# Exponentials and weighted sums over whole rows of 4096 columns, with the broadcast rows in single tiles refilled by halves

## The chip, the cores and the metric

The kernel runs on one core of one Trainium2 chip. The metric is device time in microseconds (us) for one execution, as a median of runs; lower is better. A profile of one execution gives each engine's instructions and waits: TensorE (PE, with its weight loads PEld), VectorE (DVE), ScalarE (ACT), GpSimd (POOL) and SyncE (SP), which issues most of the DMAs.

## The reference, cut to what matters

The input is 16 images of 64 x 64 positions with 256 channels, 4096 tokens an image. Four layers follow each other, each normalized per group of channels over the image, and each added to its input. Layer 0 replaces each token by the nearest of 1024 codes (the "search"). Layer 1 is a gated attention inside each image row. Layer 2, where the change lies, makes three scalars x0, x1, x2 per token, a 4096 x 4096 similarity, its softmax, and a gate:

```python
def layer2(x, w1, b1, w2, b2, w3, b3):
    x0 = jnp.einsum('bnc,c->bn', xf, w1) + b1[0]
    x1 = jnp.einsum('bnc,c->bn', xf, w2) + b2[0]
    x2 = jnp.einsum('bnc,c->bn', xf, w3) + b3[0]
    sim = x0[:, :, None] * x1[:, None, :]
    sm = jax.nn.softmax(sim, axis=1)
    feats = jnp.einsum('bn,bnm->bm', x2, sm)
    gate = jax.nn.sigmoid(feats).reshape(b, h, w, 1)
    return gate * x
```

For each of the 4096 tokens m, the sum over n of exp(x0[n] x1[m]) and the sum of the same weighted by x2[n] are needed. Layer 3 is a linear attention with four heads, an output projection and a layer norm.

## The kernel before, in words

The program is written as Python generators, one for each stage of each image: stats0 and stage1 (search), layer1, rows2 (the three scalars), stage2 (the exponentials), gate2 (the gate is applied) and stage3 (layer 3). A heap of due times (the list `tasks` at the end of the kernel) decides which generator is advanced next, so that at any time several images are in different stages; each `yield` gives a share of the stage's length, and one image takes about as long as one stage of exponentials. A scheduler below the language then sets the order of instructions on each engine by priority and readiness, inserts the waits, and gives out the buffers. Within one engine instructions run in that order.

rows2(b) loads the image's eight chunks again (L562, tile xr), multiplies them on TensorE by the three weight vectors (L565), copies the row to SBUF (L569), writes it to DRAM (`rd`, L571) and turns x0 and x1 into one column per 128 tokens (x01, L575). `spread_rows` (L582 to L590) then brings one half row, 2048 columns of x0 and of x2, back to all 128 partitions (x0b and x2b, two buffers each, 1 MB a transfer, issued on SP's queue at L587). The first half is spread at the end of rows2, the second at the start of stage2.

stage2(b) takes the extremes of x0 over partitions (L598 to L601, with a GpSimd reduction), makes the bias nmax from them (L603, L604), and then runs 64 halves: for each half row and each of 32 groups of 128 tokens, ScalarE makes the exponentials of 2048 columns and their sum den (L617), into one of three buffers `ex`, and VectorE multiplies them by x2b and sums them into num (L620). Both read a per-partition scalar or two and write an accumulator. Then den and num of the two halves are added and the gate is formed (L628 to L641). The last image runs with parts=8: 8 groups of four tokens' groups, with its gate2 stage interleaved.

The search (stage1) makes for each of the 32 token groups T the row of norms `nn` on ScalarE (L372), the products with the 1024 codes on TensorE into a PSUM tile of 1024 columns (pd, L377, from the pool ps_w with two buffers), their sum with nn and its maximum on VectorE (L384, into `nd`), the index of the maximum (L389), and a gather of codes by GpSimd (L390). The 4 KB tiles nn, nd, the squares sq (L320), fg of layer 1 (L461) and rows share one tag, t4, with five buffers. The other PSUM tiles come from a pool of four banks (ps_m), which all stages share. Other lines that are named later: L468 and L506 are layer 1's products, L511 its sum on VectorE, L857 and L865 the scaled copy and the sum at layer 3's output.

Of the kernel before, what the change touches and what calls it, by code (L numbers as in the profile page):

```python
# [9 lines left out]
F32 = mybir.dt.float32  # L10
BF16 = mybir.dt.bfloat16
U32 = mybir.dt.uint32
AF = mybir.ActivationFunctionType
ALU = mybir.AluOpType
AX = mybir.AxisListType

P = 128
C = 256
NK = C // P
TOK = 4096  # L20
NT = TOK // P
CH = 4
NCHUNK = NT // CH
CW = CH * P
# [3 lines left out]
CODES = 1024  # L28
CK = 32
# [12 lines left out]
def kernel(  # L42
# [7 lines left out]
    nc = tc.nc  # L50
# [8 lines left out]
    s1p = ctx.enter_context(tc.tile_pool(name="s1p", bufs=2))  # L59
    s2p = ctx.enter_context(tc.tile_pool(name="s2p", bufs=1))  # L60
    s3p = ctx.enter_context(tc.tile_pool(name="s3p", bufs=2))
    wts = ctx.enter_context(tc.tile_pool(name="wts", bufs=1))
    small = ctx.enter_context(tc.tile_pool(name="small", bufs=2))
# [34 lines left out]
    neg_mat = s1p.tile([P, P], F32, tag="t4", name="neg_mat", bufs=5)  # L98
# [72 lines left out]
    e_raw = s2p.tile([P, NK, CODES], F32, tag="x0b", name="e_raw", bufs=2)  # L171
# [3 lines left out]
    e_sq = s2p.tile([P, NK, CODES], F32, tag="x2b", name="e_sq", bufs=2)  # L175
# [127 lines left out]
    def stage1(b):  # L303
        tag = f"s1_{b}"
        scale, _, nbias = norm0.pop(b)
# [12 lines left out]
        def norm(ch):  # L318
            xn[ch] = s1p.tile([P, NK, CW], F32, tag="xn", name=f"xn_{tag}_{ch}")
            sq = s1p.tile([P, NK, CW], F32, tag="t4", name=f"sq_{tag}_{ch}", bufs=5)  # L320
            for k in range(NK):
                nc.scalar.activation(
                    xn[ch][:, k, :], xt[ch][:, k, :], AF.Identity, bias=nbias[:, k : k + 1], scale=scale[:, k : k + 1]
                )
                nc.scalar.activation(
                    sq[:, k, :], xt[ch][:, k, :], AF.Square, bias=nbias[:, k : k + 1], scale=scale[:, k : k + 1]
                )
            px = bank(f"px_{tag}_{ch}")
            for t in range(CH):
                for k in range(NK):  # L330
                    nc.tensor.matmul(
                        px[32 * t : 32 * t + 32, :P], lhsT=neg32, rhs=sq[:, k, t * P : (t + 1) * P],
                        start=(k == 0), stop=(k == NK - 1),
                    )
            xrow = small.tile([P, P], F32, tag="xrow", name=f"xrow_{tag}_{ch}", bufs=1)
            nc.scalar.copy(xrow, px[:, :P])
            pxt[ch] = bank(f"pxt_{tag}_{ch}")
            nc.tensor.transpose(pxt[ch][:, :P], xrow, ident)
# [28 lines left out]
        for ch in range(NCHUNK):  # L367
            for t in range(CH):
                T = ch * CH + t

                nn = s1p.tile([P, CODES], F32, tag="t4", name=f"nn_{tag}_{T}", bufs=5)
                nc.scalar.activation(nn, ne2, AF.Identity, bias=nx2[ch][:, t : t + 1])  # L372
                pd = wide(f"pd_{tag}_{T}")
                for hf in range(2):
# [7 lines left out]
                nd = s1p.tile([P, CODES], F32, tag="t4", name=f"nd_{tag}_{T}", bufs=5)  # L382
                m8 = m8s[T % 4]
                nc.vector.tensor_tensor_reduce(  # L384
                    out=nd, in0=pd, in1=nn, scale=1.0, scalar=-3.0e38, op0=ALU.add, op1=ALU.max,
                    accum_out=m8[:, 0:1],
                )
                i8 = small.tile([P, 8], U32, tag="i8", name=f"i8_{tag}_{T}", bufs=4)
                nc.vector.max_index(i8, m8, nd)  # L389
# [26 lines left out]
    def layer1(b):  # L416
# [34 lines left out]
        def attend(ch):  # L451
# [9 lines left out]
            fg = s1p.tile([2 * CK, 2, HW], F32, tag="t4", name=f"fg_{tag}_{ch}", bufs=5)  # L461
# [78 lines left out]
    def rows2(b):  # L540
# [17 lines left out]
        for h in range(2):  # L558
# [9 lines left out]
            rows = s1p.tile([P, CW], F32, tag="t4", name=f"rows_{tag}_{h}", bufs=5)  # L568
# [11 lines left out]
        rows_d[b] = x01, rd, [spread_rows(rd, b, 0)]  # L580

    def spread_rows(rd, b, h):  # L582

        x0b = s2p.tile([P, TOK // 2], F32, tag="x0b", name=f"x0b_{b}_{h}", bufs=2)
        x2b = s2p.tile([P, TOK // 2], F32, tag="x2b", name=f"x2b_{b}_{h}", bufs=2)
        for dst, n in ((x0b, 0), (x2b, 2)):
            nc.sync.dma_start(  # L587
                out=dst, in_=rd[n : n + 1, h, :, :].rearrange("o j n -> o (j n)").to_broadcast([P, TOK // 2])
            )
        return x0b, x2b  # L590

    def stage2(b, parts=1):

        tag = f"s2_{b}"
        x01, rd, halves = rows_d.pop(b)
# [6 lines left out]
        nmax = small.tile([P, NT], F32, tag="nmax", name=f"nmax_{tag}", bufs=1)  # L602
        nc.vector.tensor_scalar(nmax, x01[:, :, 1], ab[:, 0:1], -1.0, ALU.mult, ALU.mult)  # L603
        nc.vector.scalar_tensor_tensor(nmax, x01[:, :, 1], ab[:, 1:2], nmax, op0=ALU.mult, op1=ALU.min)  # L604
        den = small.tile([P, 2, NT], F32, tag="den", name=f"den_{tag}", bufs=1)
        num = small.tile([P, 2, NT], F32, tag="num", name=f"num_{tag}", bufs=1)
        halves.append(spread_rows(rd, b, 1))
# [3 lines left out]
        rest = gate2(b) if parts > 1 else None  # L611
        for part in range(parts):
            those = range(part * NT // parts, (part + 1) * NT // parts)
            for h, (x0b, x2b) in enumerate(halves):
                for T in those:
                    ex = s2p.tile([P, TOK // 2], F32, tag="ex", name=f"ex_{tag}_{h}_{T}", bufs=3)
                    nc.scalar.activation(  # L617
                        ex, x0b, AF.Exp, bias=nmax[:, T : T + 1], scale=x01[:, T, 1:2], accum_out=den[:, h, T : T + 1]
                    )
                    nc.vector.tensor_tensor_reduce(  # L620
                        out=ex, in0=ex, in1=x2b, scale=1.0, scalar=0.0, op0=ALU.mult, op1=ALU.add,
                        accum_out=num[:, h, T : T + 1],
                    )
                    yield 2.4
# [320 lines left out]
```

## Time and profile before

| What | Value |
|---|---|
| Median of three runs | 5938.17 us (5902.65 to 5948.46) |
| The profiled execution's own time | 5928.44 us |
| Its span in the profile | 5926.7 us |
| Busy: TensorE, VectorE, ScalarE, GpSimd | 5337.4, 5121.1, 4570.8, 1939.4 us |
| Granted TensorE clock, mean | 0.941 |
| DMA | 1059.47 MB, mean 179 GB/s |

The page gives busy time per engine, then the costliest groups of instructions by line: busy time and mean duration in nanoseconds of one, then the idle time of the engine just before them and who ended it. A table of stages gives the busy time of each engine (with its number of instructions) in a stretch of the span, then the granted clock, the share of time that the DMA engines were busy, and GB/s. The waits list who waited for whom: us in total, number of times, the longest. The timeline lists instructions by start and duration; the chain in order of time follows the end of the program back through what released each step.

### The profile page before, as it was taken

The numbers are of one execution on the slowest core, as the hardware profiler recorded it, in microseconds if no ns is written. First come the engines' busy times: TensorE is split into PE (matmuls) and PEld (weight loads), VectorE is DVE, ScalarE is ACT, GpSimd is POOL, SyncE is SP. The second block draws the span as 40 slices with busy tenths as digits, with TensorE's granted clock in tenths as the row PEclk, the third lists the DMA queues.
The fourth block names the chain that finished last, engine by engine and source line by source line (L and its number), as shares of the span: only waits on it lengthen the run. The fifth ranks groups of instructions, "written<-read, shape, count | busy, mean of one in ns | idle before, by whom it ended". The sixth has DMA issues, their size and how long they took to land.

```text
span 5926.7 us, 79561 instructions
## 1 busy us (share of the span) xinstructions
PE 5337.4 (90%) x28239; PEld 3211.1 (54%) x28239; DVE 5121.1 (86%) x7282; ACT 4570.8 (77%) x6754; POOL 1939.4 (33%) x1314
## 2 busy tenths in 40 slices
PE   8968899889999999998989999898999989997777
PEld 3524465545656565564656556565555646564555
DVE  6499798989989898898989889898998989888882
ACT  4377687878778787887879788797878878787873
POOL 3122233224233332433334233342424333231331
PEclk9989999989999898999999899999999999998899
DMA  6544745555656656565665656656565664644543
GB/s 186 162 124 124 225 137 177 184 184 162 207 168 192 197 151 202 184 207 181 184 205 167 194 183 188 206 174 204 164 210 164 202 204 147 209 158 173 184 158 116
DMA packets 521380, 1059.47 MB, mean 179 GB/s; under 512 B 52504, under 2 KB 266392, under 8 KB 512792
## 3 DMA queue, kind: packets, MB, share of 16 engines
q1 hardware_dynamic: 406288, 885.11, 44.7%
q0 software_dynamic: 73728, 67.14, 7.9%
q10 hardware_dynamic: 40968, 102.13, 4.5%
q8 instruction: 224, 3.67, 0.3%
q14 instruction: 172, 1.41, 0.1%
HBM read 751.18 MB, written 303.04 MB: 178 GB/s over the span
## 4 chain that ended last, share of the span: by engine, by line
PE 48%; DVE 16%; ACT 12%; DMA 7%; issue 6%; POOL 4%; ACTq 0%; SPq 0%; POOLq 0%; DVEq 0%
PE pd_s L377 15%; DVE ex_s L620 6%; ACT ex_s L617 5%; PE ph_l L468 5%; PE pqv_s L759 3%; PE po_s L854 3%; PE pk_s L737 3%; PE po_l L506 2%; PE pr_r L565 2%; DMA xr_r<-x_l 2%; DVE i_s L389 2%; POOL qv_s L779 2%; PE pvr_s L834 1%; PE pz_s L826 1%; DMA qo_s<-qd_s 1%
## 5 line engine op out<-in xcount | busy, mean ns | idle before, releaser
L620 DVE CUSTOM_DVE_ANT_0 ex_s<-ex_s,x2b 128x2048 f32<-128x2048 f32 x1024 | 2350.7, 2302 | 46.2 <-ACT ex_s L617 44.9
L617 ACT ACTIVATE ex_s<-x0b,nmax_s,x_r 128x2048 f32<-128x2048 f32 x1024 | 2137.8, 2088 | 66.4 <-DVE num_s L620 60.3
L377 PE MATMUL pd_s<-e,xn_s 128*128 128x512 f32 x4096 | 2022.2, 623 | 43.5 <-DVE m L384 40.8
L390 POOL DMA_INDIRECT xc_s<-in_emb_rows,i_s x512 | 1058.1, 2067 | 2063.9 <-DVE i_s L389 1466.8
L377 PEld LDWEIGHTS pd_s<-e,xn_s 128*128 128x128 f32 x4096 | 754.4, 197 | 764.9 <-issue 669.1
L384 DVE CUSTOM_DVE_ANT_0 nd_s<-pd_s,nn_s 128x1024 f32<-128x1024 f32 x512 | 622.2, 1215 | 174.4 <-ACT nn_s L372 82.1
L389 DVE FIND_INDEX8 i_s<-m,nd_s 128x8 uint32<-128x1024 f32 x512 | 624.1, 1219 | 0.0
L372 ACT ACTIVATE nn_s<-ne,nx_s 128x1024 f32<-128x1024 f32 x512 | 583.2, 1141 | 21.5 <-DVE nx_s L343 15.7
L468 PE MATMUL ph_l<-wh_l,xt_l 128*128 128x256 f32 x2048 | 525.5, 393 | 28.3 <-DVE m L384 16.5
L759 PE MATMUL pqv_s<-wqv_s,xk_s 128*128 128x256 f32 x2048 | 494.6, 382 | 0.0
L759 PEld LDWEIGHTS pqv_s<-wqv_s,xk_s 128*128 128x128 f32 x2048 | 390.9, 192 | 127.5 <-issue 65.5
L468 PEld LDWEIGHTS ph_l<-wh_l,xt_l 128*128 128x128 f32 x2048 | 380.9, 193 | 143.8 <-issue 57.5
L837 POOL TENSOR_TENSOR lrs_s<-lrs_s,mhalf 128x4 f32<-128x4 f32 x128 | 183.0, 1429 | 749.3 <-ACT lrs_s L836 710.5
L857 ACT ACTIVATE y_s<-po_s,lrs_s 128x256 f32<-128x256 f32 x512 | 237.1, 469 | 214.8 <-PE po_s L854 166.2
L854 PE MATMUL po_s<-wctx_s,qo_s 128*128 128x256 f32 x1024 | 336.0, 415 | 32.3 <-ACT y_s L857 31.1
L506 PE MATMUL po_l<-at_l,h_l 64*128 64x64 f32 x4096 | 318.5, 297 | 46.2 <-DVE xt_l L511 42.7
L506 PEld LDWEIGHTS po_l<-at_l,h_l 64*128 64x128 f32 x4096 | 286.5, 206 | 108.5 <-DVE xt_l L511 48.9
L779 POOL TENSOR_TENSOR qv_s<-qv_s,qm_s 128x512 f32<-128x512 f32 x128 | 232.7, 1818 | 312.3 <-DVE qm_s L778 181.7
L728 POOL TENSOR_TENSOR qv_s<-qv_s,qd_s 128x512 f32<-128x512 f32 x128 | 199.8, 1561 | 304.6 <-DVE qd_s L727 252.9
L865 DVE TENSOR_TENSOR y_s<-pxo_s,y_s 128x512 f32<-128x512 f32 x256 | 175.2, 686 | 125.0 <-ACT y_s L857 123.2
L854 PEld LDWEIGHTS po_s<-wctx_s,qo_s 128*128 128x128 f32 x1024 | 178.2, 198 | 172.5 <-ACT y_s L857 84.7
L737 PE MATMUL pk_s<-xk_s,wk_s 128*128 128x512 f32 x512 | 269.6, 650 | 0.0
(195 smaller groups left out, 7519.8 us busy)
## 6 DMA issues: line engine op xcount, KB each, us to landing
xs_s<-in_xT SPq DMA_DIRECT2D x128, 512.0 KB
xt_s<-in_xT SPq DMA_DIRECT2D x128, 512.0 KB
xc_s<-in_x SPq DMA_DIRECT2D x128, 512.0 KB
x_s<-xt_s ACTq DMA_DIRECT2D x128, 512.0 KB
xt_l<-x_s SPq DMA_DIRECT2D x128, 512.0 KB
x_l<-xt_l SPq DMA_DIRECT2D x128, 512.0 KB
xr_r<-x_l SPq DMA_DIRECT2D x128, 512.0 KB
xg_g<-x_l SPq DMA_DIRECT2D x128, 512.0 KB
```

The source lines that it names most:

```text
L372: nc.scalar.activation(nn, ne2, AF.Identity, bias=nx2[ch][:, t : t + 1])
L377: nc.tensor.matmul(pd[:, cols], lhsT=xn[ch][:, k, t * P : (t + 1) * P], rhs=e2[:, k, cols], start=(k == 0), stop=(k == NK - 1),)
L384: nc.vector.tensor_tensor_reduce(out=nd, in0=pd, in1=nn, scale=1.0, scalar=-3.0e38, op0=ALU.add, op1=ALU.max, accum_out=m8[:, 0:1],)
L389: nc.vector.max_index(i8, m8, nd)
L390: nc.gpsimd.indirect_dma_start(out=xc[ch][:, t, :], out_offset=None, in_=emb_rows, in_offset=bass.IndirectOffsetOnAxis(ap=i8[:, 0:1], axis=0),
L468: nc.tensor.matmul(ph[:, t, :], lhsT=X[:, k, t * P : (t + 1) * P], rhs=wh_n[:, k, :], start=(t % 2 == 0 and k == 0), stop=False, skip_grou ...
L506: nc.tensor.matmul(po[:, r, k * CH + t, :], lhsT=h[rows, t, k * P : (k + 1) * P], rhs=at[rows, t, :], start=True, stop=True,)
L617: nc.scalar.activation(ex, x0b, AF.Exp, bias=nmax[:, T : T + 1], scale=x01[:, T, 1:2], accum_out=den[:, h, T : T + 1])
L620: nc.vector.tensor_tensor_reduce(out=ex, in0=ex, in1=x2b, scale=1.0, scalar=0.0, op0=ALU.mult, op1=ALU.add, accum_out=num[:, h, T : T + 1],)
L737: nc.tensor.matmul(pk, lhsT=wk_n[:, k, :], rhs=xt[:, k, :], start=(k == 0), stop=(k == NK - 1))
L759: nc.tensor.matmul(pqv[:, j, :], lhsT=xt[:, k, t * P : (t + 1) * P], rhs=wqv_n[:, k, :], start=(j == 0 and k == 0), stop=False, skip_group ...
L854: nc.tensor.matmul(po[:, j, :], lhsT=qT[:, t * P : (t + 1) * P], rhs=wctx[:, 1, :], start=True, stop=True)
```

## The change: what it does

- x0b and x2b become one tile each for the whole program, 4096 columns wide with one buffer. The code book's raw values and squares at the program's start lie in them.
- One exponential and one weighted sum cover 4096 columns (`weigh`), in two buffers `ex` of 4096 columns. In all images but the last, the first four and the last four token groups are still done by halves of 2048 columns (EDGE = 4), and the half rows are refilled between them: the next image's first half of x0b after the last groups' first halves, of x2b one exponential later, the second half of x0b after the last exponential, and the second half of x2b after the first exponential of the new image.
- The spreads are issued on ScalarE's queue, not SP's, one half row of one tile at a time (`spread_row`, L598 to L605 of the changed kernel).
- The extremes and nmax (two buffers) are made at the end of rows2, with two more yields there.
- The second halves of den and num are set to zero, since whole rows write the first alone.
- In the search, the sum with the products is written over nn; nd is gone, and t4 has three buffers in place of five.

In the changed kernel the exponential is L624, the weighted sum L628, the search's sum L386, the index L391, layer 1's sum L513, and layer 3's scaled copy L893. The diff, without the hunks that only put `bufs=3` for `bufs=5` in the tag t4:

```diff
-    e_raw = s2p.tile([P, NK, CODES], F32, tag="x0b", name="e_raw", bufs=2)
+    x0b = s2p.tile([P, TOK], F32, tag="x0b", name="x0b")
+    x2b = s2p.tile([P, TOK], F32, tag="x2b", name="x2b")
+    e_raw = x0b[:, 0 : NK * CODES].rearrange("p (k n) -> p k n", k=NK)
...
-    e_sq = s2p.tile([P, NK, CODES], F32, tag="x2b", name="e_sq", bufs=2)
+    e_sq = x2b[:, 0 : NK * CODES].rearrange("p (k n) -> p k n", k=NK)
...
-                nd = s1p.tile([P, CODES], F32, tag="t4", name=f"nd_{tag}_{T}", bufs=5)
                 m8 = m8s[T % 4]
                 nc.vector.tensor_tensor_reduce(
-                    out=nd, in0=pd, in1=nn, scale=1.0, scalar=-3.0e38, op0=ALU.add, op1=ALU.max,
+                    out=nn, in0=pd, in1=nn, scale=1.0, scalar=-3.0e38, op0=ALU.add, op1=ALU.max,
                     accum_out=m8[:, 0:1],
                 )
...
-                nc.vector.max_index(i8, m8, nd)
+                nc.vector.max_index(i8, m8, nn)
...
-        rows_d[b] = x01, rd, [spread_rows(rd, b, 0)]
-
-    def spread_rows(rd, b, h):
-
-        x0b = s2p.tile([P, TOK // 2], F32, tag="x0b", name=f"x0b_{b}_{h}", bufs=2)
-        x2b = s2p.tile([P, TOK // 2], F32, tag="x2b", name=f"x2b_{b}_{h}", bufs=2)
-        for dst, n in ((x0b, 0), (x2b, 2)):
-            nc.sync.dma_start(
-                out=dst, in_=rd[n : n + 1, h, :, :].rearrange("o j n -> o (j n)").to_broadcast([P, TOK // 2])
-            )
-        return x0b, x2b
-
-    def stage2(b, parts=1):
-
-        tag = f"s2_{b}"
-        x01, rd, halves = rows_d.pop(b)
 
         ext = small.tile([P, 2], F32, tag="ext", name=f"ext_{tag}", bufs=1)
...
         nc.gpsimd.partition_all_reduce(ab, ext, P, bass_isa.ReduceOp.max)
-        nmax = small.tile([P, NT], F32, tag="nmax", name=f"nmax_{tag}", bufs=1)
+        yield 1
+        nmax = small.tile([P, NT], F32, tag="nmax", name=f"nmax_{tag}", bufs=2)
...
+        rows_d[b] = x01, nmax, rd
+        yield 1
+
+    H = TOK // 2
+    spread = set()
+
+    def spread_row(b, h, dst, n):
+
+        if (b, h, n) not in spread and b in rows_d:
+            nc.scalar.dma_start(
+                out=dst[:, h * H : (h + 1) * H],
+                in_=rows_d[b][2][n : n + 1, h, :, :].rearrange("o j n -> o (j n)").to_broadcast([P, H]),
+            )
+            spread.add((b, h, n))
+
+    def stage2(b, parts=1):
+
+        tag = f"s2_{b}"
+        for dst, n in ((x0b, 0), (x2b, 2)):
+            spread_row(b, 0, dst, n)
+        x01, nmax, _ = rows_d[b]
...
-        halves.append(spread_rows(rd, b, 1))
+        nc.vector.memset(den[:, 1, :], 0.0)
+        nc.vector.memset(num[:, 1, :], 0.0)
...
+        def weigh(T, h, first, last):
+            ex = s2p.tile([P, TOK], F32, tag="ex", name=f"ex_{tag}_{h}_{T}", bufs=2)[:, first:last]
+            nc.scalar.activation(
+                ex, x0b[:, first:last], AF.Exp, bias=nmax[:, T : T + 1], scale=x01[:, T, 1:2],
+                accum_out=den[:, h, T : T + 1],
+            )
+            nc.vector.tensor_tensor_reduce(
+                out=ex, in0=ex, in1=x2b[:, first:last], scale=1.0, scalar=0.0, op0=ALU.mult, op1=ALU.add,
+                accum_out=num[:, h, T : T + 1],
+            )
+
+        EDGE = 4
+        if parts > 1:
+            for dst, n in ((x0b, 0), (x2b, 2)):
+                spread_row(b, 1, dst, n)
         for part in range(parts):
             those = range(part * NT // parts, (part + 1) * NT // parts)
-            for h, (x0b, x2b) in enumerate(halves):
-                for T in those:
-                    ex = s2p.tile([P, TOK // 2], F32, tag="ex", name=f"ex_{tag}_{h}_{T}", bufs=3)
-                    nc.scalar.activation(
-                        ex, x0b, AF.Exp, bias=nmax[:, T : T + 1], scale=x01[:, T, 1:2], accum_out=den[:, h, T : T + 1]
-                    )
-                    nc.vector.tensor_tensor_reduce(
-                        out=ex, in0=ex, in1=x2b, scale=1.0, scalar=0.0, op0=ALU.mult, op1=ALU.add,
-                        accum_out=num[:, h, T : T + 1],
-                    )
-                    yield 2.4
+            halved = [T for T in those if parts == 1 and (T < EDGE or T >= NT - EDGE)]
+            if parts == 1:
+                for h in range(2):
+                    for T in range(EDGE):
+                        weigh(T, h, h * H, (h + 1) * H)
+                        for dst, n in ((x0b, 0), (x2b, 2)):
+                            spread_row(b, 1, dst, n)
+                        yield 2.4
+            for T in those:
+                if T not in halved:
+                    weigh(T, 0, 0, TOK)
+                    yield 4.8
+            if parts == 1:
+
+                for h in range(2):
+                    for T in range(NT - EDGE, NT):
+                        weigh(T, h, h * H, (h + 1) * H)
+                        if h == 1:
+                            spread_row(b + 1, 0, x2b, 2)
+                        yield 2.4
+                    spread_row(b + 1, h, x0b, 0)
+            rows_d.pop(b, None)
```

More of the change, by code (lines that the diff above doesn't have):

```diff
@@ L97 @@
     hmask = blocks("hmask", DH, 1.0)
-    neg_mat = s1p.tile([P, P], F32, tag="t4", name="neg_mat", bufs=5)
+    neg_mat = s1p.tile([P, P], F32, tag="t4", name="neg_mat", bufs=3)
     nc.vector.memset(neg_mat, -1.0)
@@ L319, in norm @@
             xn[ch] = s1p.tile([P, NK, CW], F32, tag="xn", name=f"xn_{tag}_{ch}")
-            sq = s1p.tile([P, NK, CW], F32, tag="t4", name=f"sq_{tag}_{ch}", bufs=5)
+            sq = s1p.tile([P, NK, CW], F32, tag="t4", name=f"sq_{tag}_{ch}", bufs=3)
             for k in range(NK):
@@ L369, in stage1 @@
                 T = ch * CH + t
-                nn = s1p.tile([P, CODES], F32, tag="t4", name=f"nn_{tag}_{T}", bufs=5)
+                nn = s1p.tile([P, CODES], F32, tag="t4", name=f"nn_{tag}_{T}", bufs=3)
                 nc.scalar.activation(nn, ne2, AF.Identity, bias=nx2[ch][:, t : t + 1])
@@ L460, in attend @@
                     )
-            fg = s1p.tile([2 * CK, 2, HW], F32, tag="t4", name=f"fg_{tag}_{ch}", bufs=5)
+            fg = s1p.tile([2 * CK, 2, HW], F32, tag="t4", name=f"fg_{tag}_{ch}", bufs=3)
             for n in range(2):
@@ L567, in rows2 @@
                     )
-            rows = s1p.tile([P, CW], F32, tag="t4", name=f"rows_{tag}_{h}", bufs=5)
+            rows = s1p.tile([P, CW], F32, tag="t4", name=f"rows_{tag}_{h}", bufs=3)
             nc.scalar.activation(rows, pr, AF.Identity, bias=brow_n)
```

## The prediction

> **What bounds the kernel now.** I read five views: the page, the table of stages, the waits by engine, the timeline of VectorE and ScalarE, and the chain in order of time. The page first:
>
> ```profile
> span 5926.7 us, 79561 instructions
> PE 5337.4 (90%) x28239; PEld 3211.1 (54%) x28239; DVE 5121.1 (86%) x7282; ACT 4570.8 (77%) x6754; POOL 1939.4 (33%) x1314
> ...
> L620 DVE CUSTOM_DVE_ANT_0 ex_s<-ex_s,x2b 128x2048 f32<-128x2048 f32 x1024 | 2350.7, 2302 | 46.2 <-ACT ex_s L617 44.9
> L617 ACT ACTIVATE ex_s<-x0b,nmax_s,x_r 128x2048 f32<-128x2048 f32 x1024 | 2137.8, 2088 | 66.4 <-DVE num_s L620 60.3
> ```
>
> No engine is alone the bound. L617 and L620, the two lines that change, are 47% of ScalarE's busy time (2137.8 of 4570.8) and 46% of VectorE's (2350.7 of 5121.1), and the engines hardly wait for each other there (46.2 and 66.4 us). The table of stages, in slices of 30 us, columns as on the page:
>
> ```profile
> 3510.00:3540.00 30.00, 29.61 (x168) 18.73 (x166) 26.98 (x38) 27.49 (x41) 16.45 (x10) 1.00 0.29 81
> 3570.00:3600.00 30.00, 29.82 (x201) 19.36 (x200) 29.75 (x42) 26.83 (x39) 14.72 (x8) 1.00 0.59 181
> 3780.00:3810.00 30.00, 26.92 (x113) 14.91 (x112) 23.28 (x40) 22.26 (x32) 7.68 (x5) 1.00 0.75 267
> ```
>
> In the middle of an image TensorE is at 99% and VectorE at 90 to 99%; where one image's exponentials hand over to the next (3780 to 3810, with L565's row sums) all three have slack. Now the waits of TensorE, VectorE and SP's queue (us in total, times, longest):
>
> ```profile
> PE pd_s L377 <- DVE m L384: 40.8, 28, 6.0
> ...
> DVE y_s L865 <- ACT y_s L857: 123.2, 81, 4.3
> ...
> DVE nd_s L384 <- ACT nn_s L372: 82.1, 59, 7.3
> ...
> SPq L587 <- DMA rows_r<-rows_r: 75.2, 17, 7.9
> ...
> SPq L587 <- DVE num_s L620: 47.3, 13, 4.4
> ```
>
> TensorE waits in many short pieces: 28 of 512 search tiles found their PSUM tile not yet emptied. VectorE mostly waits for ScalarE. Last, what one instruction costs from start to start, from the timeline, and one transfer from the chain:
>
> ```profile
> 2898.35 2.27 DVE L620 CUSTOM_DVE_ANT_0 ex_s<-ex_s,x2b 128x2048 f32<-128x2048 f32 x1
> 2900.55 0.08 DVE L620 DVE_READ_ACCUMULATOR2_ANT num_s<- 128x1 f32 x1
> 2900.55 1.22 DVE L511 TENSOR_TENSOR xt_l<-po_l,xt_l 128x1024 f32<-128x1024 f32 x1
> 2901.69 2.28 DVE L620 CUSTOM_DVE_ANT_0 ex_s<-ex_s,x2b 128x2048 f32<-128x2048 f32 x1
> ...
> 2901.20 2.10 ACT L617 ACTIVATE ex_s<-x0b,nmax_s,x_r 128x2048 f32<-128x2048 f32 x1
> ...
> 2903.28 0.81 ACT L674 ACTIVATE u_g<-gb_g,one,s_n 128x512 f32<-128x512 f32 x1
> ...
> 2908.99 3.60 PE L377 MATMUL pd_s<-e,xn_s 128*128 128x512 f32 x8
> ...
> 3796.90 6.78 DMA x2b<-rows_r
> ```
>
> On VectorE a half takes 2.20 us until the next instruction starts (2898.35 to 2900.55), its accumulator read included, and 1024 columns take 1.14 (2900.55 to 2901.69): records overlap, and the fixed part is small. On ScalarE a half takes 2.08 (2901.20 to 2903.28). One spread of a half row is in flight for 6.8 us.
>
> [...] the median record of L620 is 2282. [...] L377's mean record is 623 ns, but eight of them end within 3.60 us, 450 ns each. TensorE's 99% thus hides some slack.
>
> **The change part by part.** Count: the first 15 images have 64 halves each; now the first four and last four rows stay halved (16 halves) and 24 rows are whole. The last image has 32 whole rows. So 15 x 24 + 32 = 392 pairs become one instruction on each engine.
>
> VectorE: 2048 further columns cost at least 2 x 1.06 (2.20 less 1.14 for 1024), so a whole row takes about 4.33 and saves 2 x 2.20 - 4.33 = 0.07. By records it would be 0.15 and a read of 0.083, 0.23. I take 0.07, since the next instruction starts before the record ends: 392 x 0.07 = 27 us (upper end 90). VectorE is busy in mid-image, so it counts in full.
>
> ScalarE: no 4096-column form is in the trace. [...] By the trace alone (L372 starts the next after 1.10 for 1024 columns, so 0.98 per 1024) a whole row is 4.04 and saves 0.12. I take 0.38, [...]: 392 x 0.38 = 149 us (lower end 47). ScalarE isn't the bound; its gain comes as shorter waits. VectorE's idle time put down to ScalarE is 123.2 + 82.1 and seven smaller rows of the same view, together 378 us. ScalarE's busy share falls from 77.1 to 74.6%, busy to idle from 3.37 to 2.94; if waits go with that ratio they fall 13%, 49 us.
>
> Longer instructions: a whole row holds VectorE 2.13 us longer than a half (4.33 - 2.20) and ScalarE 1.71 (3.79 - 2.08). What TensorE needs from behind such a row comes late by half of that on average, 1.07 and 0.86. If a share f of the 392 rows on each engine has something urgent behind it, the price is f x 392 x 1.93 = 757 f. From the waits, 28 of 512 search tiles are urgent today, f = 0.055: 41 us. The lower bound is nothing (order is re-made by the scheduler); the upper one is in the rivals.
>
> The refill: x0b and x2b lose their second buffers. The spreads (64 of 0.32 to 0.42 us to issue) go from SP's queue to ScalarE's, where the next exponentials, copies out of PSUM and stores stand behind them. In the order that the scheduler makes, x2b's first half stands behind the old image's last exponential, and from image 3 to 13 it names no wait for VectorE (the two ex buffers have made that wait already), only for earlier transfers. Between it and the next image's first exponential stand some 3.5 us of ScalarE work; with that exponential 5.6, against 6.8 for the transfer: VectorE waits 1.2 us, x 11 = 13. The last image needs all four pieces at once, 7 more: 20 us together (0 if other work fills it, 102 if it doesn't, below). What SP no longer waits for (75.2 + 47.3) frees loads that run ahead anyway: 0; what is late next on SP are its own buffer waits.
>
> Edits at nothing: two 32-column memsets an image (3 us on VectorE in all, by the 0.1 us of L603) against the 4.2 us that exponentials waited for nmax, now made in rows2, on POOL too, which is 33% busy. Search: nn is overwritten in place and t4 has 3 buffers, not 5; a search tile took two of five and now takes one of three, held until L389 ends; alone that allows more tiles in flight, but if sq and fg hold two, L372 waits for L389, and ScalarE stands. I put that in the range.
>
> Sum: -27 - 49 + 41 + 20 = -15 us on the profiled execution's own 5928.44 (its span 5926.7 and 1.7 around it), 5913. The median of the runs, 5938.17, lies 10 above it; between the two bases I say 5915.
>
> **The rivals.** *Whole rows block TensorE* (slower). Same savings, but f is one in five: 757 / 5 = 151, -76 + 20 + 151 = +95, 6023. It decides from f = 56/757, one in 13, on. For it: PSUM has only two wide tiles and four banks for all stages, and every wait of TensorE in its list is on an evacuation, a normalization or a load. Against it: total work ahead of an evacuation is the same, and only its grain is coarser.
> *ScalarE's saving arrives in full* (faster): -149 + 20 = -129, 5799. For it: VectorE's waits for ScalarE, and ScalarE at 92% in the slice at 3510. Against it: 77% on average.
> *The refill comes late* (the row isn't there when it is wanted): 15 hand-overs x 6.8 = 102 in place of 20, -76 + 41 + 102 = +67, 5995. For it: the 6.78 us piece in the chain. Against it: four halved rows on each side cover about 4 x 2.2 us of it.
>
> **How the numbers follow.** Forecast 0.38, with its own range 5850 to 5985; TensorE blocked 0.32; saving in full 0.22; late refill 0.08. A measurement here tells 1% (59 us) from no change at best. Faster by over 1%: a third of the forecast (0.12), nearly all of the full saving (0.21), 0.01 of the rest, 0.34. Slower: 0.04 of the forecast, 0.26 of blocking, 0.05 of the late refill, 0.35. Within: 0.31. The range takes in the full saving and the blocking case up to f = 0.24: 5790 to 6055.
>
> **What would show it.** Right: L628 at about 4.4 us and L624 at about 3.8 for whole rows, ScalarE's busy time down by some 150, VectorE's waits for ScalarE down by a tenth, TensorE's waits for L386 up by a fifth or less. Wrong, slower: TensorE's waits for L386, L893 and L513 grow by over 100 us together. Wrong, faster: these stay, and the mid-image period falls by 5 us or more an image. The late refill would show as VectorE or ScalarE waiting for x2b or x0b transfers.

## The result and the profile after

The changed kernel takes 6250.49 us (median of four runs, 6221.0 to 6262.6), against 5940.53 for four runs of the kernel before: a ratio of 1.0536, interval 1.0486 to 1.0586. It is 310 us slower. The forecast was 5915, and 6250 lies outside its range.

The page of the changed kernel, in the lines that answer to those shown of before (busy time of each engine, the chain that ended last by engine, the two lines of the exponentials):

```profile
span 6246.4 us, 77989 instructions
...
PE 5425.2 (87%) x28239; PEld 3243.8 (52%) x28239; DVE 5106.9 (82%) x6530; ACT 4429.3 (71%) x5970; POOL 2252.7 (36%) x1314
...
PE 40%; DVE 17%; ACT 15%; POOL 9%; issue 8%; DMA 5%; ACTq 0%; POOLq 0%; SPq 0%; DVEq 0%
...
L628 DVE CUSTOM_DVE_ANT_0 ex_s<-ex_s,x2b 128x4096 f32<-128x4096 f32 (+1 forms) x632 | 2297.2, 3641 | 88.2 <-ACT ex_s L624 86.3
...
L624 ACT ACTIVATE ex_s<-x0b,nmax_r,x_r 128x4096 f32<-128x4096 f32 (+1 forms) x632 | 1988.5, 3147 | 43.7 <-DVE num_s L628 40.6
```

VectorE and ScalarE do less work, as the change intends: 14 us and 141.5 us less. Yet the span is 320 us longer. GpSimd has exactly as many instructions as before (1314) and is busy 313 us longer (1939.4 to 2252.7), although the change touches none of its additions and multiplications. Its share of the chain rises from 4% to 9%, while TensorE's falls from 48%. The same line of before:

```profile
PE 48%; DVE 16%; ACT 12%; DMA 7%; issue 6%; POOL 4%; ACTq 0%; SPq 0%; POOLq 0%; DVEq 0%
```

The tile views give minimum, median and maximum of one instruction in nanoseconds. Three GpSimd lines of before, and below them the same three of after:

```profile
L779 POOL TENSOR_TENSOR qv_s<-qv_s,qm_s x128: 1037/1051/3173, 819.1 to 5861.3; 128x512 f32<-128x512 f32 x128
L837 POOL TENSOR_TENSOR lrs_s<-lrs_s,mhalf x128: 1006/1040/3144, 1016.2 to 5918.3; 128x4 f32<-128x4 f32 x128
L390 POOL DMA_INDIRECT xc_s<-in_emb_rows,i_s x512: 1533/1614/3692, 44.0 to 5219.9; - x171
```

```profile
L815 POOL TENSOR_TENSOR qv_s<-qv_s,qm_s x128: 1037/1048/5347, 860.0 to 6184.6; 128x512 f32<-128x512 f32 x128
L873 POOL TENSOR_TENSOR lrs_s<-lrs_s,mhalf x128: 1006/1040/5277, 1067.2 to 6238.0; 128x4 f32<-128x4 f32 x128
L392 POOL DMA_INDIRECT xc_s<-in_emb_rows,i_s x512: 1533/1606/5623, 45.2 to 5492.2; - x171
```

Minimum and median are the same before and after, to 8 ns. It is the long ones that get longer: the maximum moves by 1.9 to 2.2 us, and a whole row holds VectorE 2.1 us longer than a half. Even an instruction on four columns (L873) took up to 5.3 us. The timeline (start, duration, engine, instruction) shows how:

```profile
2248.07 4.36 DVE L628 CUSTOM_DVE_ANT_0 ex_s<-ex_s,x2b 128x4096 f32<-128x4096 f32 x1
2248.30 5.03 POOL L764 TENSOR_TENSOR qv_s<-qv_s,qd_s 128x512 f32<-128x512 f32 x1 [6.28 <-DVE qd_s L763]
...
2256.44 4.41 DVE L628 CUSTOM_DVE_ANT_0 ex_s<-ex_s,x2b 128x4096 f32<-128x4096 f32 x1
2256.53 5.23 POOL L815 TENSOR_TENSOR qv_s<-qv_s,qm_s 128x512 f32<-128x512 f32 x1 [1.19 <-DVE nx_s L346]
...
2261.79 0.63 ACT L816 ACTIVATE qv_s<-qv_s 128x512 f32<-128x512 f32 x1 [2.60 <-POOL qv_s L815]
```

L764 starts 0.23 us after a weighted sum and ends 0.9 us after it (2253.33 against 2252.43): a GpSimd instruction whose median is 1.05 us has waited for the whole sum. At 2256.53 the same happens to L815, and ScalarE stands 2.60 us for it. The waits of after, and then those of before that answer to the two GpSimd ones and to TensorE's on L325 (the scaling of a search tile; its line before is L322):

```profile
ACT qv_s L816 <- POOL qv_s L815: 209.2, 77, 8.9
...
DVE nn_s L386 <- PE pd_s L380: 122.1, 95, 11.6
...
DVE y_s L901 <- ACT y_s L893: 117.5, 86, 4.3
...
PE pd_s L380 <- ACT xn_s L325: 107.0, 23, 6.2
...
DVE ex_s L628 <- ACT ex_s L624: 86.3, 55, 5.0
...
DVE nn_s L386 <- ACT nn_s L375: 67.8, 58, 2.8
...
ACT y_s L893 <- POOL lrs_s L873: 63.6, 44, 3.7
...
PE pd_s L380 <- DVE m L386: 53.5, 36, 5.1
```

```profile
ACT qv_s L780 <- POOL qv_s L779: 144.8, 103, 3.6
...
ACT y_s L857 <- POOL lrs_s L837: 40.1, 35, 4.7
...
PE pd_s L377 <- ACT xn_s L322: 2.3, 1, 2.3
```

Added over each engine's list of waits, ScalarE stands 386 us for GpSimd (227 before), VectorE 82 (43), TensorE 38 (17). VectorE stands 473 us for ScalarE (379 before) and 512 for TensorE (350), and TensorE 811 in all (579). TensorE's busy time and its waits fill its span, so these 232 us, and 88 us more of busy TensorE for the same 28239 matmuls (5337.4 to 5425.2, at a mean granted clock of 0.918 in place of 0.941), are the 320 us of the span.

TensorE's own waits for GpSimd are small. What grew is its waits for ScalarE, from 239 to 485 us, and the largest of them, L325, is not GpSimd's alone. Eleven of its 23 waits are 6.2 us long; in the one that ends at 2156.26, ScalarE had a half row and other stages' work ahead of L325, and no wait for GpSimd. Eleven are 3.3 us long; in the one that ends at 2196.39, ScalarE had stood 2.24 us for L815 and then made a whole row.

### The profile page after: what moved, and what is told of

The parts are those of the page before. It is cut to its first block, busy times and chain, and to the rows that moved or that the text cites. A ratio compares the mean times of both kernels' runs of the same rounds, so it can differ in the third digit from the quotient of the medians.

```text
span 6246.4 us, 77989 instructions
## 1 busy us (share of the span) xinstructions
PE 5425.2 (87%) x28239; PEld 3243.8 (52%) x28239; DVE 5106.9 (82%) x6530; ACT 4429.3 (71%) x5970; POOL 2252.7 (36%) x1314
## 4 chain that ended last, share of the span: by engine, by line
PE 40%; DVE 17%; ACT 15%; POOL 9%; issue 8%; DMA 5%; ACTq 0%; POOLq 0%; SPq 0%; DVEq 0%
PE pd_s L380 15%; DVE ex_s L628 8%; ACT ex_s L624 7%; POOL xc_s L392 3%; PE po_s L890 3%; POOL qv_s L815 2%; PE ph_l L470 2%; PE po_l L508 2%; PE pr_r L567 2%; DVE i_s L391 2%; PE pqv_s L795 2%; DMA xr_r<-x_l 2%; ACT nn_s L375 2%; PE pk_s L773 2%; POOL s_n L273 2%
## 5 line engine op out<-in xcount | busy, mean ns | idle before, releaser
L628 DVE CUSTOM_DVE_ANT_0 ex_s<-ex_s,x2b 128x4096 f32<-128x4096 f32 (+1 forms) x632 | 2297.2, 3641 | 88.2 <-ACT ex_s L624 86.3
L380 PE MATMUL pd_s<-e,xn_s 128*128 128x512 f32 x4096 | 2129.7, 652 | 165.9 <-ACT xn_s L325 107.0
L624 ACT ACTIVATE ex_s<-x0b,nmax_r,x_r 128x4096 f32<-128x4096 f32 (+1 forms) x632 | 1988.5, 3147 | 43.7 <-DVE num_s L628 40.6
L392 POOL DMA_INDIRECT xc_s<-in_emb_rows,i_s x512 | 1111.9, 2172 | 1951.5 <-DVE i_s L391 1292.4
L380 PEld LDWEIGHTS pd_s<-e,xn_s 128*128 128x128 f32 x4096 | 789.4, 207 | 953.9 <-issue 720.7
L386 DVE CUSTOM_DVE_ANT_0 nn_s<-pd_s,nn_s 128x1024 f32<-128x1024 f32 x512 | 621.0, 1215 | 218.3 <-PE pd_s L380 122.1
L391 DVE FIND_INDEX8 i_s<-m,nn_s 128x8 uint32<-128x1024 f32 x512 | 623.2, 1218 | 0.3 <-issue 0.3
L873 POOL TENSOR_TENSOR lrs_s<-lrs_s,mhalf 128x4 f32<-128x4 f32 x128 | 241.9, 1890 | 641.7 <-ACT lrs_s L872 597.3
L893 ACT ACTIVATE y_s<-po_s,lrs_s 128x256 f32<-128x256 f32 x512 | 236.6, 470 | 294.5 <-PE po_s L890 162.2
L815 POOL TENSOR_TENSOR qv_s<-qv_s,qm_s 128x512 f32<-128x512 f32 x128 | 299.6, 2341 | 260.2 <-DVE qm_s L814 150.7
L764 POOL TENSOR_TENSOR qv_s<-qv_s,qd_s 128x512 f32<-128x512 f32 x128 | 230.8, 1803 | 439.5 <-DVE qd_s L763 375.4
L355 PE MATMUL pt_s<-ident,xc_s 128*128 128x128 f32 x1024 | 161.4, 290 | 149.3 <-DMA xc_s<-in_emb_rows,i_s 98.1
```

The source lines that it names most:

```text
L380: nc.tensor.matmul(pd[:, cols], lhsT=xn[ch][:, k, t * P : (t + 1) * P], rhs=e2[:, k, cols], start=(k == 0), stop=(k == NK - 1),)
L386: nc.vector.tensor_tensor_reduce(out=nn, in0=pd, in1=nn, scale=1.0, scalar=-3.0e38, op0=ALU.add, op1=ALU.max, accum_out=m8[:, 0:1],)
L391: nc.vector.max_index(i8, m8, nn)
L392: nc.gpsimd.indirect_dma_start(out=xc[ch][:, t, :], out_offset=None, in_=emb_rows, in_offset=bass.IndirectOffsetOnAxis(ap=i8[:, 0:1], axis=0),
L624: nc.scalar.activation(ex, x0b[:, first:last], AF.Exp, bias=nmax[:, T : T + 1], scale=x01[:, T, 1:2], accum_out=den[:, h, T : T + 1],)
L628: nc.vector.tensor_tensor_reduce(out=ex, in0=ex, in1=x2b[:, first:last], scale=1.0, scalar=0.0, op0=ALU.mult, op1=ALU.add, accum_out=num[: ...
```

## The experiments

Theory 1 in the expectations is what this reading suggests: the longer weighted sums shut GpSimd out, and what follows from GpSimd comes late. Against it stand the change's other parts and, later, the mere order of the instructions. Each expectation says which theories it tells apart. All ratios are to the kernel before, in the same session on the chip; its median was 5924 to 5941 us over the sessions, which ran on several chips, so a difference in us between two sessions can be off by up to 17 us.

**The parts of the change, one at a time.** The first kernel is before with only the search's edit (sum in place, three buffers in t4):

```diff
-    ... tag="t4", ..., bufs=5)
+    ... tag="t4", ..., bufs=3)
-                    out=nd, in0=pd, in1=nn, ...
+                    out=nn, in0=pd, in1=nn, ...
```

> The kernel before with one part of the change alone: the search's sum is written over nn and t4 has three buffers. If the loss of the change (310 us) comes from long rows (on VectorE, ScalarE or through GpSimd), this stays within 1% of before, 5890 to 5990 us. If the rival holds that the three buffers tie search, layer 1 and the norms together, it loses 100 us or more, 6040 or above.

Measured: 6091.73, ratio 1.0253 (1.0205 to 1.0302). An edit that I had counted at nothing goes with 151 us. The second is the changed kernel with every row by halves:

```diff
-        EDGE = 4
+        EDGE = NT // 2
...
+            for h in range(2 if parts > 1 else 0):
+                for T in those:
+                    weigh(T, h, h * H, (h + 1) * H)
```

> The changed kernel with all rows done by halves of 2048 columns again, the last image's too; single tiles refilled by halves, spreads on ScalarE's queue, nmax in rows2 and t4 stay. If the long rows are the cause, this is back near before, 5900 to 6000 us, and GpSimd's busy time falls from 2253 to about 1950 us. If refill, queue and nmax are the cause, it stays at 6150 us or above.

Measured: 6168.57, 1.0379 (1.0328 to 1.0430). GpSimd is busy 1904.6 us, about as before the change, and its longest instructions are as short as before:

```profile
L815 POOL TENSOR_TENSOR qv_s<-qv_s,qm_s x128: 1037/1048/3183, 858.0 to 6108.9; 128x512 f32<-128x512 f32 x128
```

Yet only 82 of the 310 us come back. The third and fourth keep whole rows on one engine alone, ScalarE in the third and VectorE in the fourth. The third's edit is shown; the fourth does the same to the exponentials:

```diff
+            size = min(last - first, H)
+            cuts = range(0, last - first, size)
...
-            nc.vector.tensor_tensor_reduce(
-                out=ex, ...
+            for n, at in enumerate(cuts):
+                nc.vector.tensor_tensor_reduce(
+                    out=ex[:, at : at + size], ...
+                    accum_out=num[:, h + n, T : T + 1],
```

> The changed kernel, but only ScalarE works on whole rows: VectorE sums each row's two halves by two instructions (VectorE's work as in the kernel before). Theory 1, VectorE's long rows do the harm [...]: this comes near before or below it, 5850 to 5980, with GpSimd busy about 1950 us. Rival 2, long rows on ScalarE keep TensorE waiting for evacuations: it stays at 6150 or above. If both grains count alike, it lies halfway, about 6090.

> The changed kernel, but only VectorE works on whole rows: ScalarE makes each row's exponentials by two instructions of 2048 columns. Theory 1 (VectorE's long rows shut GpSimd out): as slow as the change or slower, since ScalarE's saving is gone, 6230 to 6330 us, with GpSimd busy about 2250 us. Rival 2 (ScalarE's grain): back near before, 5900 to 6000. Halfway, about 6100, if both count alike.

Measured: 6163.3 (1.0377, 1.0327 to 1.0427) with ScalarE whole, and 6106.58 (1.0276, 1.0226 to 1.0325) with VectorE whole. Both times that theory 1 gave are missed. GpSimd's busy time follows VectorE's grain as theory 1 says: 1925.1 us where VectorE goes by halves, 2167.3 where it takes whole rows. The time doesn't follow: of these two the one with whole rows on VectorE is the faster. The wait lists go with that: in it ScalarE stands 225 us for GpSimd, less than with ScalarE whole (277) or by halves (257), so GpSimd's longer instructions did not become longer waits of ScalarE there. Why not is open.

Three more take the parts further. The first is the kernel before with the search's sum in place and the five buffers kept (of the diff above only the lines on nn). The second has the refill, ScalarE's queue and nmax in rows2 alone: halves throughout, `ex` in three buffers of 2048, the search as before. The third is the changed kernel with nmax made in stage2 again:

```diff
-            ex = s2p.tile([P, TOK], F32, tag="ex", ..., bufs=2)[:, first:last]
+            ex = s2p.tile([P, H], F32, tag="ex", ..., bufs=3)
```

```diff
-        rows_d[b] = x01, nmax, rd
+        rows_d[b] = x01, None, rd
...
-        x01, nmax, _ = rows_d[b]
+        x01, _, _ = rows_d[b]
+        ext = small.tile([P, 2], F32, tag="ext", name=f"ext_{tag}", bufs=1)
...
```

> The kernel before with the search's sum written over nn, but five buffers in t4 as before. Three buffers cost 158 us (2.5%). Theory 3, too few buffers: with five this is back at before, 5900 to 5970 us. Rival 4, the sum in place itself (nn held until the index is found, and an order that no longer fits) does it: 6050 or above.

> Of the change the single tiles refilled by halves, the spreads on ScalarE's queue and nmax in rows2 alone: all rows by halves in three buffers of 2048, search with nd and five t4 buffers as before. The same with the changed search lost 235 us, of which the search alone lost 158. If the parts add, this is at about 6010 (+77); if the loss with the changed search hides or doubles this part, at 5940 or at 6100 and above.

> The changed kernel with the extremes and nmax at the start of stage2 again. Theory: the hand-over loses because VectorE's and GpSimd's steps for nmax now stand behind the late row loads, ahead of the old image's last rows, on engines that run in order: about 70 us come back, 6180. Rival: nmax is not what is late (the row sums are waited for anyway): within 30 us of the change, 6220 to 6280.

Measured: five buffers 6085.62 (1.0273, 1.0244 to 1.0302), so the number of buffers is not what the search's edit costs. The refill alone 6154.41 (1.0367, 1.0342 to 1.0391). nmax moved back 6238.79 (1.0511, 1.0472 to 1.0549), the same as the whole change within the interval. Search (2.5%) and refill (3.7%) are together in the kernel by halves (which has two buffers `ex` where the refill's kernel has three), and that costs 3.8%: the parts don't add.

Next, the search's `nn` with two buffers of its own, and whole rows with the search as before, for whose space `ex` is in bfloat16 (its exponentials are rounded):

```diff
-                nn = s1p.tile([P, CODES], F32, tag="t4", ..., bufs=5)
+                nn = s1p.tile([P, CODES], F32, tag="nn", ..., bufs=2)
```

```diff
-            ex = s2p.tile([P, TOK], F32, tag="ex", ..., bufs=2)[:, first:last]
+            ex = s2p.tile([P, TOK], BF16, tag="ex", ..., bufs=2)[:, first:last]
```

> Search's sum in place as in the change, but nn has two buffers of its own, and squares, fg and rows keep three: nn can run at most two tiles ahead. Theory 3b, that nn runs ahead of the sums and takes ScalarE at the wrong time: back to 5900 to 5980 us. Theory 5, any new order: 6050 to 6150.

> The changed kernel with search as before (nd, five buffers in t4); the room comes from exponentials and products kept as bf16 in ex (rounded, the sums still fp32). If the search's buffers are a loss of its own, 158 us come back and this is at about 6090; if whole rows are the loss once more than the halves show, it stays above 6200; if whole rows only hurt together with three buffers, it falls to 5950 to 6020.

Measured: own buffers 6031.82 (1.0179, 1.0147 to 1.0211), between its two expectations. Whole rows without the search's edit 6283.12 (1.0590, 1.0559 to 1.0621): taking the edit out of the change gives nothing back (a whole row takes VectorE and ScalarE as long in bfloat16, 4407 and 3787 ns at the median, against 4406 and 3789). An edit that goes with 151 us alone and with nothing in company is no steady cost.

**What the order alone is worth.** Two edits of the kernel before change no instruction, buffer or queue, only the due times: one constant of a stage's lag, and the length that the search is said to have.

```diff
-LAG2 = 0.17
+LAG2 = 0.18
```

```diff
-        task("search", b, 1.0, stage1(b), 160)
+        task("search", b, 1.0, stage1(b), 161)
```

> The kernel before with another neutral edit: the exponentials are due 0.01 of an image (3.5 us) later (LAG2 0.18). It re-orders more than the first (1105 neighbours on ScalarE). Theory 5: 6050 to 6150 us. Rival: 5880 to 5990.

> The kernel before with a neutral edit: the search's length is divided into 161 parts, not 160, so that due times shift by under 1% and the scheduler makes another order of the same instructions, with the same buffers and queues. ScalarE's order then has 807 places where two neighbours stand the other way round than before, as many as with the search's sum in place (801). Theory 5, the order before is an unusually good one and any new order costs 2 to 3%: 6050 to 6120 us. Rival, the parts of the change cost by what they do: within 1% of before, 5880 to 5990.

Measured: 5989.17 (1.0098, 1.0067 to 1.0128), within what its expectation gives the rival, and 6129.98 (1.0353, 1.0318 to 1.0389), just above the range of theory 5. The pages have the same instructions on each engine as before, the second for instance:

```profile
PE 5389.5 (88%) x28239; PEld 3244.9 (53%) x28239; DVE 5152.2 (84%) x7282; ACT 4563.7 (75%) x6754; POOL 1992.8 (33%) x1314
```

So 49 and 189 us come from nothing but another order of the same work; the kernel before stands in a better one than these two. The search's edit (2.5, 2.7 and 1.8% in its three forms) lies inside this scatter, and the refill (3.7%) just above the larger of the two. A single comparison can't say what they cost in themselves. The same two edits on the changed kernel, and the first on the kernel by halves:

> The changed kernel with the exponentials due 0.01 of an image later. If orders of one kernel scatter by some 2% and before stands at the good end, this lies anywhere from 6150 to 6330 us, and a shift of over 40 us from 6250 shows the scatter. If times go by what the kernels do, it stays within 30 us of 6250.

> The changed kernel with the search's length divided into 161 parts. The same edit cost the kernel before 200 us. If the change is slow by what it does, this lies at 6200 to 6400 us. If its order was only unlucky, some orders come near before, and this may fall below 6150.

> All rows by halves in the refilled tiles, with the exponentials due 0.01 of an image later. The first order took 6169 us; the same shift made the kernel before 58 us slower and the change 103 us slower. If whole rows cost by themselves, this stays 80 us or more below the change in the same order (6353). If all is scatter of orders, it can lie on either side of 6353.

Measured: whole rows 6353.2 (1.0713, 1.0683 to 1.0743) with the lag and 6171.2 (1.0424, 1.0384 to 1.0465) with 161; halves 6096.97 (1.0284, 1.0248 to 1.0319) with the lag. Compared under the same settings, the change costs 310 us as it stands, 364 with the lag (6353.2 - 5989.2) and 41 with 161 (6171.2 - 6130.0). It is slower three times in three, but by how much depends on the order (with 161, 6171.2 lies between its two expectations). The traces of the three pairs show what goes with that (us, changed kernel less kernel before):

| Order | The change costs | GpSimd busy | ScalarE's waits for GpSimd | TensorE's waits |
|---|---|---|---|---|
| as it stands | +310 | +313 | +159 | +232 |
| LAG2 0.18 | +364 | +126 | +123 | +269 |
| 161 | +41 | +22 | +17 | +44 |

Where the change costs little, GpSimd hardly waits longer. But with the lag it costs most and GpSimd waits less than half as much more, so GpSimd's busy time is no measure of the loss. Whole rows against halves cost 82 us as they stand (6250.5 - 6168.6) and 256 with the lag.

**GpSimd let in.** If GpSimd's waiting is how whole rows do their harm, a VectorE instruction of the same length that leaves GpSimd alone must do none. That a sum with one operand in SBUF in place of two is such an instruction was an assumption that no run had tried by then. These kernels leave out the weighting by x2b and only sum the exponentials, so they don't compute the gate:

```diff
-            nc.vector.tensor_tensor_reduce(
-                out=ex, in0=ex, in1=x2b[:, first:last], scale=1.0, scalar=0.0, op0=ALU.mult, op1=ALU.add,
-                accum_out=num[:, h, T : T + 1],
-            )
+            nc.vector.tensor_reduce(num[:, h, T : T + 1], ex, AX.X, ALU.add)
```

> The changed kernel, but VectorE sums ex alone (the weighting by x2 is left out), one SBUF operand and about the same 4.4 us for a row. Theory 1, GpSimd stands while VectorE reads two operands: GpSimd's busy time falls from 2253 to below 1700 us, and the time from 6250 to about 6150 (that of halves) or lower. Theory 2, the grain itself: GpSimd's busy time falls too, but the time stays at 6200 to 6350.

> All rows by halves in the refilled tiles, and VectorE sums ex alone (the weighting is left out), 2.2 us for a half. The counterpart of whole rows with one operand. Theory 1: little is left between the two, within 60 us of each other. Theory 2: whole rows stay 80 us or more above this one. With two operands the halves took 6169 us; if GpSimd's standing costs them too, this is below 6120.

> Whole rows with one operand (weighting left out) in another order (exponentials due 0.01 of an image later). With two operands the same shift moved whole rows from 6250 to 6353. Theory 1: below 6220. Theory 2: 6250 to 6400.

> Halves with one operand (weighting left out) in that other order. Scatter of orders alone: within 100 us of the first order of halves with one operand, and under Theory 2 again 80 us or more below whole rows in the same order; under Theory 1 within 60 us of them.

| VectorE reads | Order | Whole rows | Halves | Whole less halves |
|---|---|---|---|---|
| ex and x2b | as it stands | 6250.49 (1.0536) | 6168.57 (1.0379) | +82 |
| ex and x2b | LAG2 0.18 | 6353.20 (1.0713) | 6096.97 (1.0284) | +256 |
| ex alone | as it stands | 5892.50 (0.9925, 0.9898 to 0.9951) | 6026.02 (1.0160, 1.0123 to 1.0196) | -134 |
| ex alone | LAG2 0.18 | 6050.64 (1.0193, 1.0157 to 1.0230) | 5983.79 (1.0098, 1.0068 to 1.0129) | +67 |

From the tile views of the kernel with whole rows that sums ex alone, and from its timeline and page:

```profile
L628 DVE TENSOR_REDUCE num_s<-ex_s x632: 2226/4401/4427, 331.0 to 5654.3; 128x1 f32<-128x4096 f32 x98, 128x1 f32<-128x2048 f32 x60
```

```profile
L812 POOL TENSOR_TENSOR qv_s<-qv_s,qm_s x128: 1038/1050/1660, 832.7 to 5835.6; 128x512 f32<-128x512 f32 x128
```

```profile
2147.16 4.36 DVE L628 TENSOR_REDUCE num_s<-ex_s 128x1 f32<-128x4096 f32 x1
2147.38 1.05 POOL L761 TENSOR_TENSOR qv_s<-qv_s,qd_s 128x512 f32<-128x512 f32 x1 [6.25 <-DVE qd_s L760]
```

```profile
PE 5279.8 (89%) x28239; PEld 3172.2 (54%) x28239; DVE 5056.8 (86%) x5898; ACT 4429.2 (75%) x5970; POOL 1347.8 (23%) x1314
```

VectorE is held as long as in the changed kernel: 4401 ns for a whole row, against this row of the changed kernel:

```profile
L628 DVE CUSTOM_DVE_ANT_0 ex_s<-ex_s,x2b x632: 2226/4406/5558, 328.9 to 6020.1; 128x4096 f32<-128x4096 f32 x98, 128x2048 f32<-128x2048 f32 x60
```

But at 2147.38 a GpSimd instruction that starts 0.22 us after such a sum takes 1.05 us, where the like of it took 5.03. The sum also writes no `ex` back any more, but the write is not what held GpSimd: in the changed kernel the search's sum L386 writes a whole tile (1024 columns, 1.16 us) and reads one operand from SBUF and one from PSUM, and L764 beside it (2895.11 and 2895.34) takes 1.05 us. So GpSimd's standing goes with the second operand in SBUF here: the longest of the 128 instructions on qv_s shown above took 5347 ns beside sums with it (L815) and 1660 without (L812). GpSimd is busy 1348 us for the same instructions: by this difference, an estimate, 905 of its 2253 us in the changed kernel were waiting, and 592 of 1939 in the kernel before. VectorE seems to lose at times too: its longest sum is 5.56 us with x2b and 4.43 without.

What follows for the time: taking the second operand away gives whole rows 358 and 303 us, halves 143 and 113 (6168.6 - 6026.0, 6097.0 - 5983.8). Whole rows lose 215 us more to it than halves in the one order and 189 in the other, and without it they are on average no slower than halves. The times for whole rows are those of theory 1 (below 6150 and 6220), but whole rows and halves were to lie within 60 us of each other, and they lie 134 apart one way and 67 the other.

This fits GpSimd shut out for 4.4 us as the greater part of what whole rows cost against halves, and speaks against the grain alone; it doesn't settle it. The four kernels also don't wait for x2b's refill and don't write ex, so these go into the 303 to 358 as well. Each difference carries an order scatter of the size measured above (among these four, the lag alone moves whole rows by 158 us and halves by 42), so that only the agreement of the two orders speaks for 200 us. And the kernel with whole rows on VectorE alone stands against it: GpSimd waits there too (2167.3 us busy), yet it is 62 us faster than all halves. That is within what the order alone moved, and stays open.

## Why the prediction was wrong

- **The fused instructions: right.** 392 pairs are fused (1024 less 632). A whole row holds VectorE 4.34 us from start to start (2256.44 to 2260.78; I had 4.33) and its median on ScalarE is 3.79. I had 3.78 for it, and so 0.38 saved a pair (2 x 2.08 - 3.78), an assumption that no view of before showed; by its trace alone a whole row was 4.04. ScalarE saves 141.5 us of busy time (I had 149), VectorE 14 (27).
- **ScalarE's saving as shorter waits, -49: wrong in sign.** VectorE's waits for ScalarE rose from 379 to 473 us. The step assumed that waits go with ScalarE's busy share. ScalarE is less busy, but it stands 159 us longer for GpSimd; that VectorE's longer waits stand behind this is argued, not measured.
- **Longer instructions, 757 f with f = 0.055: wrong in its cause.** I priced what TensorE needs from behind a long row on VectorE and ScalarE, and gave signs for that. They didn't come: TensorE's waits for L386 are 64 us over all lines (60 before), for L893 73 (52), and for L513 they fell from 55 to below 2. The step that failed is the list of who is held: it has what stands behind the row on its own engine, and not GpSimd, which stands beside it and for which the sum had no term. In its place the runs show GpSimd held behind the weighted sums and 313 us busier, and ScalarE standing 159 us longer for it; how many of the 310 us that makes is not settled. The rival "whole rows block TensorE" had the direction (6023). Its wait on ScalarE did grow, by 247 us in all, but most of it at lines that the prediction hadn't named, L325 first (2.3 to 107), and behind waits for GpSimd and half rows as well as whole ones.
- **The evidence was in the profile of before.** L779 had a mean of 1818 ns and a median of 1051, L837 a mean of 1429 for four columns. ScalarE's list of waits, which I didn't show, had 227 us for GpSimd. I read GpSimd as 33% busy and left it there. From those rows the missing term could have been bounded: a GpSimd instruction waited up to about the length of one weighted sum (the longest L779 took 3173 ns, 2122 above its median; a sum takes 2282 at the median), and the change about doubles this length (4406).
- **The refill, 20: not settled.** The direct wait isn't there: for the spreads, the list of waits has 0.6 us before L624 and none before L628. Two other waits go with it. VectorE's for its loads (DMA) are 49 to 61 us in all fourteen kernels with the refill and 15 to 22 in the six without. TensorE's for L325 are 56 to 112 us in thirteen of the fourteen, also where the sum reads ex alone (70 to 81), and 2 to 17 in the six without; with 161, where the change costs only 41 us, they are 20. I had put what SP no longer waits for at 0 and had no term for TensorE at the hand-over. So a part of the loss may be the refill's order and not GpSimd's. The kernels with the refill and halves are 108 to 228 us slower than before under the same settings (6097.0 - 5989.2; 6168.6 - 5940.5). With the scatter this can't be put down to the refill, the search or the order.
- **The search and nmax at nothing.** nmax: right (6238.79 against 6250.49 with it moved back). Search: open; alone it stands at +91 to +151 us, inside the scatter, and without it the change is no faster.
- **The range.** Its terms were 20 to 50 us each, and it had no term for the order that the scheduler makes. Two empty edits of the kernel before moved it by 49 and 189 us. Terms of this size can't carry a forecast of 5915 with an upper end of 6055; the range should have had the scatter on its upper side.

## What to carry to other kernels

Before making a VectorE instruction with two SBUF operands longer, look for GpSimd rows whose mean lies well above their median: here (L779, mean 1818 ns, median 1051) they were waiting behind such instructions already, and then waited up to about as long as the new one lasts (5347 ns at most, beside rows of 4406). Then look at who stands for GpSimd in the other engines' waits, since GpSimd's busy time alone did not foretell the loss (313 us more of it went with 310 us, 126 with 364). Where a scheduler orders several stages by due times, shift one due time by a hair and measure first (here that moved the kernel before by 49 and 189 us): differences below what that moves are not yet effects of an edit, and a comparison is worth more under two or three such orders. No version here that does the weighting is faster than the kernel before.

## What the runs showed of the hardware

- One weighted sum on VectorE with both operands in SBUF held up GpSimd instructions of 1.05 us to as much as 5.35 us (L815), a multiplication of four columns (1.04 to 5.28 us) and the gather's issue (1.6 to 5.6 us) alike; beside a sum of the same 4.4 us with one operand, the longest on the same line (L812 there) was 1.66, and the longest gather's issue 1.90. I had not expected a third of GpSimd's busy time in the kernel before (592 of 1939 us, the estimate above) to be waiting.
- The same instructions in another order took 1.0 and 3.5% longer, with intervals of about 0.3% to each side. TensorE's mean granted clock fell broadly as the time rose over all profiled runs, from 0.942 in the 5903 us of whole rows on ex alone to 0.915 in the 6365 us of the changed kernel with the lag. Whether the lower clock is a part of the cause or follows from the gaps was not tried.
